# The store of a graph network's output, issued from ScalarE's queue in place of SyncE's

## The chip, the core and the metric

The kernel runs on one core of a Trainium2 chip. A core has TensorE (matrix products; PE in the profile, with its weight loads as PEld), VectorE (DVE), ScalarE (ACT), GpSimd (POOL) and SyncE (SP). Each works through its own queue of instructions in order, and they wait for one another through semaphores. Transfers between the chip's memory (DRAM) and the on-chip buffers run on 16 DMA engines; an engine of the core issues a transfer and goes on, and the transfer raises a semaphore when it has landed. The metric is the device time of one execution, in microseconds (us), median of several.

## The reference, cut to what matters

Sixty-four graphs of 256 nodes with 256 features each go through two layers; nothing connects one graph with another. All is in 32-bit floats.

```
layer 0:  h = gat(gat(x, adj, W1, a1), adj, W2, a2)      # gat: softmax over masked pair scores, times h W
          h = layernorm(x + h)
          x = layernorm(h + relu(h w_ff1 + b) w_ff2 + b)
layer 1:  attn = softmax(q k^T / sqrt(32)), 8 heads      # q, k = x Wq + bq, x Wk + bk
          out  = sum over relations r of (attn * (adj == r)) v_r
          x = layernorm(x + out Wo + bo)
          x = layernorm(x + gelu(x W1 + b1) W2 + b2)     # this is the output
```

`adj` has entries of 0 and 1 only, which the kernel makes use of, and checks: a general version of the whole computation follows behind a branch that these inputs don't take.

## The kernel before, in words

`binary` does the work. For each graph `b` the function `graph` makes a dictionary of small pieces of program, named by stage and step: G (the two graph-attention steps), F (the first feed-forward block), A (the attention), T (the end: projection, layernorm, second feed-forward block, last layernorm, store), L (loads). A piece is a few instructions. Which piece is run when is written out by hand: START fills a pipeline, PERIOD is run 58 times, each entry with a lag that says to which graph it belongs (in the period that starts graph n, `T.out/6` is the store of graph n-6), and END empties the pipeline. About seven graphs are in work at once. The order of pieces is the order of instructions on every engine; the scheduler adds none of its own.

Pieces and names that matter here:

- The store is `T.out`, function `store`, L1147: 256 KB from the tile `res_d` to the output, a transfer of 128 partitions x 2 rows of 1 KB. It stands in PERIOD behind `A.oc0` and ahead of `A.rz11`, `G.rzA`, `F.r3` and `F.r2`, and 6 times in END, the last three as `T.rbD:-3 T.rbD:-2 T.out:-3 T.rsD:-1 T.out:-2 T.nmD:-1 T.rbD:-1 T.out:-1`.
- `res_d` is written by `T.rbD` (`finished`, L613 and L614, VectorE), the weight and bias of the last layernorm. Its input `n_d` is written by ScalarE (`norm_to`, L591) in `T.nmD`.
- The pool `work` holds three buffers with the tag `res`. They are shared by `res_d` and by the scaled rows `res_a`, `res_b` and `res_c`, which GpSimd writes in `scaled`: L629 (times the weight, two instructions) and L634 (plus the bias). A buffer is written anew only when its last reader is done.
- GpSimd's order around the store is: the division by the sums of the softmax (L1057), `res_a` (`F.raA`, `F.rbA`), the root of the variance of the next layernorm (`T.rsC`, `rstd_c`, L583), and the sums of the hidden blocks of the feed-forward (`F.u0`, `F.u1`, `F.u3`, `F.u2`; tile `H_a`, L676), which TensorE multiplies at L796.
- ScalarE's order around the store is: the copies `oT` of the attention's result (`A.oc1`, `A.oc0`, L1095), the division `whz_A` (`G.rzA`, L923), the relu on the tile `hid_a` (`F.r3`, `F.r2`, L776), the copy `wh_B` (`G.wd1`, L864), the variance `var_c` (`T.lnC`, L579).
- All other transfers of the loop are issued by SyncE: the loads of `xT`, `adj` and `x` (L359, L363, L373), and the transposes through DRAM, which `turned` makes of a VectorE transpose of 32 x 32 blocks, a store `far...` (L546) and four loads (L553). Pieces named `dt`, `dm` and `mg` are these three steps. ScalarE issues two transfers in the whole kernel, both in the setup (L400).

What the weights of seven block products do in place of eight (`seven_products`) is of no account here.

Of the kernel before, what the change touches and what calls it, by code (L numbers as in the profile page):

```python
# [34 lines left out]
P = 128  # L35
# [175 lines left out]
def binary(ctx: ExitStack, tc: tile.TileContext, t, most, out: bass.AP):  # L211

    nc = tc.nc
# [409 lines left out]
    def scaled(do, stage, key, name, tiles, g, b):  # L623


        def times():
            tiles["res"] = work.tile([P, NT, D], F32, tag="res", name=f"res_{name}", bufs=3)
            for i in range(NT):
                nc.gpsimd.tensor_tensor(  # L629
                    tiles["res"][:, i, :], tiles["y"][:, i, :], rows[g], ALU.mult  # L630
                )

        def plus():
            nc.gpsimd.tensor_tensor(tiles["res"], tiles["res"], over_nodes(b), ALU.add)  # L634

        do[f"{stage}.ra{key}"], do[f"{stage}.rb{key}"] = times, plus

    def to_columns(do, stage, key, name, tiles, pairs=False):

        def out():
            sq = work.tile([P, 4, NT * KC * 32], F32, tag="sq", name=f"sq_{name}", bufs=2)
            flat = sq.rearrange("p b n -> p (b n)")
            if pairs:
                return flat, sq.rearrange("p b (t r k) -> p t k b r", t=NT, k=KC)
            return flat, flat

        def rows():
            y = tiles["y"]  # L650
            if pairs:
                return y.rearrange("p t (k b c) -> p t k b c", k=KC, b=4)
            return y.rearrange("p t (k b c) -> p b (t k) c", k=KC, b=4)

        def into():
            cols = work.tile([P, KC * N], F32, tag="cols", name=f"cols_{name}", bufs=3)
            if pairs:
                tiles["cols"] = cols.rearrange("p (n k) -> p k n", k=KC)
            else:
                tiles["cols"] = cols.rearrange("p (a t k r) -> p k t a r", a=4, t=NT, k=KC)  # L660
            return cols.rearrange("p (a n) -> p a n", a=4)

        turned(do, stage, key, f"y_{name}", P, rows, into, out)
# [14 lines left out]
    def combine(do, stage, key, name, tiles):  # L678


        def sums():
            s = tiles["S"] = work.tile([P, 4, P], F32, tag="S", name=f"S_{name}", bufs=3)
            cols = tiles["cols"]
            blocks = [block(cols, c, i) for i in range(NT) for c in range(KC)]
            sums = [s[:, n, :] for n in range(4)]
            if len(blocks[0].shape) == 3:
                sums = [n.rearrange("p (a r) -> p a r", a=4) for n in sums]
            add_sums(nc.gpsimd, blocks, sums, range(4))

        do[f"{stage}.s{key}"] = sums  # L690
# [435 lines left out]
    def graph(b, do, tiles):  # L1126
        a = gat(do, b, tiles)
        to_columns(do, "F", "A", f"a{b}", a)
        scaled(do, "F", "A", f"a{b}", a, "L0_gnn_g_ln1", "L0_gnn_b_ln1")
        combine(do, "F", "A", f"a{b}", a)  # L1130
        feed_forward(do, "F", f"a{b}", a, lambda: ff0, "r", AF.Relu)
        y = layernorm(do, "F", "B", f"b{b}", lambda: (a["ff"],), scalar=True)
        to_columns(do, "F", "B", f"y{b}", y, pairs=True)
        scaled(do, "F", "B", f"b{b}", y, "L0_gnn_g_ln2", "L0_gnn_b_ln2")
        combine(do, "F", "B", f"y{b}", y)
        heads = attention(do, b, projections(do, b, y), tiles)
        c = layernorm(do, "T", "C", f"c{b}", lambda: (heads["wo"], y["res"]))
        to_columns(do, "T", "C", f"c{b}", c)
        scaled(do, "T", "C", f"c{b}", c, "L1_gnn_g1", "L1_gnn_beta1")
        combine(do, "T", "C", f"c{b}", c)  # L1140
        feed_forward(do, "T", f"c{b}", c, ff1, "ge", AF.Gelu, b >= B - LAST)
        d = layernorm(
            do, "T", "D", f"d{b}", lambda: (c["ff"],), ("L1_gnn_g2", "L1_gnn_beta2"), True
        )

        def store():
            nc.sync.dma_start(out=out[b].rearrange("(t p) d -> p t d", p=P), in_=d["res"])  # L1147

        do["T.out"] = store

# [16 lines left out]
    with tc.manual_schedule(engines={E.PE, E.DVE, E.Activation, E.Pool, E.SP}):  # L1167
        for entry in START:
            piece, b = entry.split(":")
# [4 lines left out]
        for entry in END:  # L1174
            piece, b = entry.split(":")
# [306 lines left out]
```

## Time and profile before

| | |
|---|---|
| median of 3 runs | 2996.35 us (2993.79 to 2996.53) |
| profiled execution | 2993.21 us, of which the span from first to last instruction 2991.4 us |
| TensorE's granted clock | 0.995 of full speed |
| busy: TensorE / weight loads / VectorE / ScalarE / GpSimd | 99% / 89% / 87% / 75% / 76% |
| transfers | 449.27 MB in 401891 packets, 150 GB/s; SyncE's queue takes 46.7% of 16 engines' span |
| the store L1147 | 64 issues, 372 to 400 ns each, landing 2.1 to 4.0 us after issue, median 2.2 |

The page gives busy times by engine, the chain of work that ended last, the costliest groups of instructions and the issues of transfers. The timeline lists instructions of one engine in order of time: start and duration in us, engine, line, operation, the tile written and the tiles read, how many were merged, and in brackets how long the engine was idle before and whose work ended that. The view of a tile lists what writes and reads it, with durations as min/median/max in ns, and the time from issue to landing for a transfer. The list of waits says who waited for whom, how long in total, how often and how long at most.

### The profile page before, as it was taken

The page shows a single profiled execution, that of the slowest core. Times are in us where ns is not written, and L with a number is a line of the kernel's source. Part 1 is how long each engine was busy: PE and PEld are TensorE (multiplying, and loading weights), DVE is VectorE, ACT ScalarE, POOL GpSimd, SP SyncE. Part 2 cuts the span into 40 slices and gives each one's busy share as a digit, 9 for nine tenths or more (in the row PEclk, how much of TensorE's full clock was granted, in tenths as well). Part 3 has the DMA queues.
Part 4 walks back from the last instruction along what each step waited for, and adds up shares of the span by engine and source line. Part 5 has one row for each costly group of instructions (what it writes and reads, how often), then busy time and mean ns, then how long its engine had stood idle before and what let it go on. Part 6 is the DMA issues. An engine that isn't in the chain of part 4 may idle for free.

```text
span 2991.4 us, 75422 instructions
## 1 busy us (share of the span) xinstructions
PE 2947.1 (99%) x25662; PEld 2672.7 (89%) x25662; DVE 2599.5 (87%) x6247; ACT 2232.7 (75%) x6404; POOL 2281.8 (76%) x3455
## 2 busy tenths in 40 slices
PE   8999999999999999999999999999999999999997
PEld 7889999989999999999899899999999998898985
DVE  4888888888889888888898898898888898888885
ACT  3677787787787777777777777777877877877764
POOL 6777777777777777777778778777777787777785
PEclk9999999999999999999999999999999999999999
DMA  5545445445445444444444454454454444444442
GB/s 140 156 149 160 149 150 155 155 146 159 150 152 158 148 149 155 149 152 155 151 155 153 153 156 150 152 159 145 150 161 150 149 158 150 147 158 148 135 156 86
DMA packets 401891, 449.27 MB, mean 150 GB/s; under 512 B 41152, under 2 KB 342720, under 8 KB 401504
## 3 DMA queue, kind: packets, MB, share of 16 engines
q1 hardware_dynamic: 399984, 442.14, 46.7%
q8 instruction: 209, 3.42, 0.5%
q0 software_dynamic: 976, 1.72, 0.3%
q14 instruction: 178, 1.46, 0.2%
q10 hardware_dynamic: 544, 0.52, 0.1%
HBM read 242.90 MB, written 201.33 MB: 148 GB/s over the span
## 4 chain that ended last, share of the span: by engine, by line
PE 90%; POOL 3%; DVE 2%; DMA 2%; issue 1%; SPq 1%; ACT 0%; POOLq 0%; DVEq 0%; ACTq 0%
PE hX_a L758 8%; PE o L1082 8%; PE fX_a L796 7%; PE fX_c L796 7%; PE hX_c L758 7%; PE sc L1024 5%; PE wo L1103 4%; PE hY_a L758 4%; PE qX L967 4%; PE fY_c L796 4%; PE hY_c L758 4%; PE fY_a L796 3%; PE gat_a L930 3%; PE gat_b L930 3%; PE wh L847 3%; PE vX L991 3%
## 5 line engine op out<-in xcount | busy, mean ns | idle before, releaser
L1071 DVE SCALAR_TENSOR_TENSOR pm<-away,pm 128x512 f32<-128x512 uint8 x512 | 356.8, 708 | 4.4 <-DMA pm<-far_p 4.0
L542 DVE STREAM_TRANSPOSE p<-p 128x1024 f32<-128x1024 f32 x256 | 315.4, 1232 | 4.1 <-POOL p L1057 4.1
L1082 PE MATMUL o<-pm,v 128*32 128x256 f32 x4096 | 235.9, 381 | 0.0
L776 ACT ACTIVATE hid_c<-hid_c,col_L_gnn_b 128x256 f32<-128x256 f32 x512 | 231.5, 505 | 1.8 <-DVE hid_c L734 0.4
L776 ACT ACTIVATE hid_a<-hid_a,col_L_gnn_b_ff 128x256 f32<-128x256 f32 x512 | 224.2, 501 | 2.4 <-DVE hid_a L734 2.2
L796 PE MATMUL fX_a<-f_L_gnn_w_ff,hid_a 128*128 128x128 f32 x1536 | 203.8, 276 | 1.7 <-DVE acc_a L734 1.3
L796 PEld LDWEIGHTS fX_a<-f_L_gnn_w_ff,hid_a 128*128 128x128 f32 x1536 | 196.0, 192 | 10.5 <-DVE acc_a L734 2.4
L796 PE MATMUL fX_c<-f_L_gnn_W,hid_c 128*128 128x128 f32 x1536 | 203.5, 275 | 0.8 <-DVE acc_c L734 0.4
L1082 PEld LDWEIGHTS o<-pm,v 128*32 128x32 f32 x4096 | 126.6, 110 | 85.7 <-DVE pm L1071 1.1
L796 PEld LDWEIGHTS fX_c<-f_L_gnn_W,hid_c 128*128 128x128 f32 x1536 | 191.8, 192 | 5.6 <-DVE acc_c L734 0.6
L676 POOL TENSOR_TENSOR S_y<-cols_y 128x128 f32<-128x128 f32 x128 | 66.3, 518 | 121.1 <-DMA cols_y<-far_y_y 120.8
L770 ACT COPY hid_a<-hX_a 128x512 f32<-128x512 f32 x192 | 113.1, 589 | 60.5 <-PE hX_a L758 60.2
L1024 PE MATMUL sc<-kT,qT 32*128 32x256 f32 x2048 | 146.7, 400 | 2.5 <-DVE kT L988 2.4
L864 ACT COPY wh_B<-gat_a 128x258 f32<-128x258 f32 x124 | 46.3, 374 | 133.5 <-PE gat_a L930 133.5
L758 PE MATMUL hX_a<-S_a,f_L_gnn_w_ff 128*128 128x128 f32 x1024 | 144.1, 284 | 0.0
L758 PEld LDWEIGHTS hX_c<-cols_c,f_L_gnn_W 128*128 128x128 f32 x1024 | 131.0, 191 | 13.1 <-DVE hid_c L734 3.1
L758 PEld LDWEIGHTS hX_a<-S_a,f_L_gnn_w_ff 128*128 128x128 f32 x1024 | 124.0, 191 | 19.7 <-issue 19.2
L758 PE MATMUL hY_c<-S_c,f_L_gnn_W 128*128 128x128 f32 x1024 | 139.5, 279 | 0.0
L758 PE MATMUL hX_c<-cols_c,f_L_gnn_W 128*128 128x128 f32 x1024 | 135.3, 275 | 2.9 <-DVE hid_c L734 2.5
L796 PE MATMUL fY_a<-f_L_gnn_w_ff,H_a 128*128 128x128 f32 x1024 | 137.3, 277 | 0.8 <-DVE acc_a L809 0.6
L796 PE MATMUL fY_c<-f_L_gnn_W,H_c 128*128 128x128 f32 x1024 | 136.0, 276 | 1.5 <-POOL H_c L676 0.9
L758 PE MATMUL hX_a<-cols_a,f_L_gnn_w_ff 128*128 128x128 f32 x1024 | 136.0, 276 | 0.4 <-DMA cols_a<-far_y_a 0.3
(2844 smaller groups left out, 10562.5 us busy)
## 6 DMA issues: line engine op xcount, KB each, us to landing
far_p<-p SPq DMA_DIRECT2D x256, 512.0 KB, 3.0
pm<-far_p SPq DMA_DIRECT2D x1024, 128.0 KB, 3.0
adj<-in_adjT SPq DMA_DIRECT2D x64, 256.0 KB, 3.4
far_y_a<-sq_a SPq DMA_DIRECT2D x64, 256.0 KB, 2.1
cols_a<-far_y_a SPq DMA_DIRECT2D x256, 64.0 KB, 2.0
far_y_y<-sq_y SPq DMA_DIRECT2D x64, 256.0 KB, 2.0
cols_y<-far_y_y SPq DMA_DIRECT2D x256, 64.0 KB, 2.0
far_y_c<-sq_c SPq DMA_DIRECT2D x64, 256.0 KB, 2.0
```

The costliest lines, as they stand in the source:

```text
L542: nc.vector.transpose(to, rows)
L758: nc.tensor.matmul(ps[:, f * P : (f + 1) * P], weights()[0][:, factor, f * P : (f + 1) * P], left, start=start and f == 0, stop=f == FC // ...
L770: nc.scalar.copy(hidden(i, h), ps.rearrange("p (f n) -> p f n", n=P))
L776: nc.scalar.activation(tiles["hid"][:, f, :], tiles["hid"][:, f, :], func, bias=b1[:, f : f + 1])
L796: nc.tensor.matmul(ps, left[:, f, :], weights()[2][:, factor, f * P : (f + 1) * P], start=start and f == 0, stop=f == FC // 2 - 1, skip_gr ...
L847: nc.tensor.matmul(t["whp", j], tiles["xT"][:, c, nodes(j)], wx[:, c, :], start=(c == 0), stop=(c == KC - 1),)
L930: nc.tensor.matmul(ps, t["s"][:, j, nodes(i)], t["whz"][:, j, :width], start=(j == 0), stop=(j == NT - 1),)
L967: nc.tensor.matmul(ps[:, nodes(n)], w[:, factor, :], right, start=start and n == 0, stop=n == 1, skip_group_check=True,)
L1024: nc.tensor.matmul(t["sc", g, hh][:, i, :], qkv["q"][hd, g, nodes(i)], qkv["k"][hd, g, :], start=True, stop=True,)
L1071: nc.vector.scalar_tensor_tensor(pm[:, 1], tiles["away"].rearrange("p (a n) -> p a n", a=4), 0.0, pm[:, 0], ALU.is_equal, ALU.mult,)
L1082: nc.tensor.matmul(ps[hh * DH : (hh + 1) * DH, :], qkv["v"][:, j, d0 : d0 + DH], t["pm", (g, hh)][:, r].rearrange("p a (j t r) -> p j t a ...
L1103: nc.tensor.matmul(t["wo"][:, i, :], t["oT"][:, c, nodes(i)], late["wo"][:, c, :], start=(c == 0), stop=(c == KC - 1),)
```

## The change

The store is issued by ScalarE. Its place in the orders START, PERIOD and END, the tile that it reads and everything else stay.

```diff
@@ -1144,7 +1144,7 @@
         def store():
-            nc.sync.dma_start(out=out[b].rearrange("(t p) d -> p t d", p=P), in_=d["res"])
+            nc.scalar.dma_start(out=out[b].rearrange("(t p) d -> p t d", p=P), in_=d["res"])
 
         do["T.out"] = store
```

## The prediction, made before the change was run

> **What bounds the kernel now.** I read the page's table of engines and its chain first, then one period of the loop engine by engine.
>
> ```profile
> PE 2947.1 (99%) x25662; PEld 2672.7 (89%) x25662; DVE 2599.5 (87%) x6247; ACT 2232.7 (75%) x6404; POOL 2281.8 (76%) x3455
> PE 90%; POOL 3%; DVE 2%; DMA 2%; issue 1%; SPq 1%; ACT 0%; POOLq 0%; DVEq 0%; ACTq 0%
> ```
>
> TensorE is busy for 99% of the span and carries 90% of the chain that ended last: only what makes a matmul start later costs time. The output's 64 issues follow one another at a median of 45.12 us (58 in the written period, 6 in END); I take the period whose output is issued at 1526.45 us, and call that moment 0. First SyncE's queue in the timeline, then the view of the tile `out`:
>
> ```profile
> 1518.88 0.47 SPq L373 DMA_DIRECT2D x<-in_x  x1
> 1526.45 0.38 SPq L1147 DMA_DIRECT2D out<-res_d  x1
> 1528.39 0.34 SPq L546 DMA_DIRECT2D far_p<-p  x1
> ```
>
> ```profile
> L1147 SPq DMA_DIRECT2D out<-res_d x64: 372/384/400, 215.3 to 2984.6; - x64
> ...
>   POOL res_a L629: 0.4, 2
> ...
> DMA to landing us min/median/max: 2.1/2.2/4.0
> ```
>
> SyncE finishes with x at 1519.35 and stands until VectorE has written `res_d` at 1526.42. The output lands 2.15 us after its issue, but up to 4.0 in some periods, and GpSimd's `res_a` (L629) is seen to wait for it: the ring of three `res` buffers gives `res_a` the buffer that the output is read from. In one period the landing at 3.97 is followed by `res_a` at 4.04, so the wake-up takes 0.07. Now ScalarE and GpSimd around the same place:
>
> ```profile
> 1529.01 0.47 ACT L1095 ACTIVATE oT<-o,col_bv 128x256 f32<-128x256 f32 x1 [0.41 <-PE o L1082]
> 1529.38 0.90 ACT L923 ACTIVATE whz_A<-wh_A,grz_A 128x258 f32<-128x258 f32 x2
> ...
> 1532.85 0.37 ACT L864 COPY wh_B<-gat_a 128x258 f32<-128x258 f32 x1 [0.98 <-PE gat_a L930]
> ```
>
> ```profile
> 1530.29 1.41 POOL L629 TENSOR_TENSOR res_a<-y_a,row_L_gnn_g_ln 128x256 f32<-128x256 f32 x2
> 1531.78 1.27 POOL L634 TENSOR_TENSOR res_a<-res_a,row_L_gnn_b_ln 128x512 f32<-128x512 f32 x1
> 1534.40 0.70 POOL L583 TENSOR_TENSOR rstd_c<-var_c,neghalf 128x2 f32<-128x2 f32 x1 [1.35 <-ACT var_c L579]
> ...
> 1537.76 1.27 POOL L676 TENSOR_TENSOR H_a<-hid_a,H_a 128x512 f32<-128x512 f32 x1
> ```
>
> ```profile
> 1539.08 0.97 PEld L796 LDWEIGHTS fY_a<-f_L_gnn_w_ff,H_a 128*128 128x128 f32 x8
> ```
>
> GpSimd goes `res_a`, `rstd_c`, then three sums `H_a` without a gap. The third ends at 1539.03, and TensorE's weight load for `fY_a` starts 0.05 later, in all 58 periods that I compared. So GpSimd's chain has no slack against TensorE, and the idle 1.35 us ahead of `rstd_c` is the only cushion behind `res_a`.
>
> **What the change does, part by part.**
>
> *SyncE loses 64 issues of 0.384 us and the stand before them.* Value: nothing. The next entry of its queue, `far_p` at 1528.39, waits for VectorE's transpose of `p` (1527.14 + 1.23 = 1528.37), not for the output. A gain is bounded by what TensorE loses in the whole periodic part beyond 45.11 us a period: 6.5 us, nearly all of it at `qX<-cols_y`, a transfer issued 20 us earlier.
>
> The Trainium skill's "DMA: Bandwidth & Descriptors", section "Issuing engines are not separate DMA queues", says that a second issuing engine saves only the sequencer's issue time. By that the sum would be 0, since SyncE stands idle anyway; the row of `res_a` says that it isn't the whole sum.
>
> *ScalarE gains 64 issues.* In its order the output stands behind the second `oT` copy (piece A.oc0) and ahead of `whz_A`. Its own two transfers in the setup took 0.44 and 0.49 us. Its queue starts a semaphore instruction 5 ns after the start of an activation still running (1534.029 after 1534.024), so I take the issue at 1529.05, +2.60, while `oT` runs. Neither semaphore holds it: `res_d` was ready at -0.03, and SyncE's separate wait for the transfer's counter (63 instructions) took 17 ns each. Queued behind it are `whz_A`, the relu on `hid_a`, and `wh_B`. `whz_A` and the relu slide by 0.1 to 0.5 us; TensorE loads `whz_A` only at 1531.56 (it was done at 1530.28), and the 0.98 us idle ahead of `wh_B` takes up the rest. Cost: nothing. Without that cover it would be 0.5 us a period, 28 us.
>
> *The output lands later, and `res_a` with it.* The issue moves from 0 to +2.60. For `rstd_c` to be on time, `res_a` may start up to 3.83 + 1.35 = 5.18, so the output must land by 5.18 - 0.07 = 5.11, or 2.51 us after ScalarE's issue. Alone it would land at 2.60 + 2.15 = 4.75: 0.36 us to spare. But it is no longer alone. The transfers' view from 1526 to 1532 in forty slices of 0.15 us:
>
> ```profile
> DMA  0000000006999930000005999989891100400000
> ```
>
> Output (0.9 us, first), then `far_p` (1.3 us, from 2.7 to 4.05). Moved, the output's data would start at 3.5 inside `far_p`'s. If the 16 engines share them with nothing lost, both are done at 2.75 + 1.3 + 0.85 = 4.9 and the output lands 0.4 later, at 5.3: `res_a` is 0.2 too late. If sharing costs the output nothing, 0. I take the middle, 0.1 us for an ordinary period.
>
> The same page, section "Queues, rings and completion order", has the engines go round-robin between queue rows packet by packet. By that the two share; the 36 ordinary periods below would cost 7 us, not 4.
>
> *Collisions with instruction fetches.* In 18 of 58 periods the output now lands at 3.3 to 4.0, since a 16 KB fetch (the page's instruction queue q8, 209 of them) sits on one of its engines; the cushion hides all of them now. `far_p`, whose time slot the output moves into, lands over 0.35 us late in 20 of 58 periods; about 13 of these are its own, and 8 or 9 more fetches start just behind it, where the output's tail will be. I take 22 periods. A collided output lands about 1.46 later than 2.15 (mean of the 18), hence at 6.2: 1.1 too late; `far_p`'s collisions cost it only 0.65, hence 5.4: 0.3. I take 0.8.
>
> *The end.* END puts T.out of graph 62 ahead of the last normalisation (T.nmD:-1).
>
> ```profile
> 2981.64 3.38 SPq L1147 DMA_DIRECT2D out<-res_d  x3
> ...
> 2981.99 1.17 ACT L591 ACTIVATE n_d<-H_c,mv_d,rstd_d 128x256 f32<-128x256 f32 x2 [0.31 <-POOL mv_d L587]
> ...
> 2983.19 0.70 DVE L613 TENSOR_TENSOR n_d<-n_d,row_L_gnn_g 128x512 f32<-128x512 f32 x1
> ```
>
> ScalarE would now stand until `res_d` of 62 is written (2983.14), issue (0.4), and start the last `n_d` at 2983.55, not 2981.99. VectorE takes `n_d` up as soon as it is there: +1.6 us on the end. The other four of END find `res_d` written, or ScalarE idle (next work at 2859.61, 2914.12, 2976.92): nothing.
>
> **Sum.** A late `res_a` shifts `rstd_c`, the `H_a` sums and `fY_a` one for one, and TensorE has no idle time in which to make it good, so each period is longer by it. 36 x 0.1 + 22 x 0.8 + 1.6 = 3.6 + 17.6 + 1.6 = 22.8 us. The profiled execution took 2993.21 (span 2991.4 and 1.8 around it), 3.1 below the median of the runs, 2996.35. On the median: 2996.35 + 22.8, about **3019 us**, +0.8%.
>
> **Rivals.**
>
> *The spare holds (not slower).* If sharing costs the output nothing and collisions keep it below 2.51 us after its issue, `res_a` is on time everywhere and only the end is left: 2996.35 + 1.6 = 2998. For it: 0.36 us of spare, and 39 of 58 outputs now land at 2.14 to 2.23. Against: `far_p` is in flight in every period, and 18 collided landings above 3.3. It decides at exactly 2.51 us from issue to landing.
>
> *ScalarE issues only when `oT` has ended.* Then +0.47 us on every landing: 36 x 0.57 + 22 x 1.27 + 1.6 = 50 us, 3046. Against it: the 5 ns above. For it: no transfer in this trace is issued beside a running activation.
>
> *SyncE's freedom pays (faster).* `x`, `far_p` or the loads would have to start earlier, but each has its own wait; at most 6.5 us, 2990.
>
> *The move changes nothing but a name.* If the two queues fed one order of transfers, `far_p` would go first in full and the output land at 4.05 + 0.85 + 0.4 = 5.3, the upper end of the ordinary period: 36 x 0.2 + 17.6 + 1.6 = 26 us, inside the forecast.
>
> **How the numbers follow.** 0.2%, or 6 us, is about what a measurement of this kernel can tell from no change. Forecast (+6 to +45): 0.60. Issue after `oT`, or worse sharing (+40 to +65): 0.14. The spare holds: 0.22. Faster: 0.04. All but the ends: 2994 takes in the spare's case, 3056 the late issue's. Slower 0.74, same 0.22, faster 0.04.
>
> **What would show it.** In the profile after: the output on ScalarE's queue 0.05 us behind the start of the second `oT`; GpSimd waiting for `out<-res_d` at `res_a` by about 1 us in nearly all periods, not 0.4 us in two; a shorter or vanished idle time ahead of `rstd_c`; matmuls of `fY_a` waiting for GpSimd's `H_a`; a period above 45.12 us, unevenly so, longest where the output lands beyond 3 us. I am wrong if landing stays below 2.5 us after issue, if `whz_A` or `wh_B` becomes the wait, or if TensorE loses its time elsewhere.

## The result, and the profile after

The changed kernel takes 3029.36 us (median of 4 runs, 3026.07 to 3030.91) against 2996.44 us before (2993.79 to 2996.76): the ratio is 1.0113, with a 95% interval of 1.0101 to 1.0125, or 33 us. It is slower, as forecast, and by ten microseconds more than the forecast of 3019 us. The profiled execution took 3029.0 us with a span of 3027.2 us, 35.8 more than the span before.

The page of the changed kernel, busy times and chain:

```profile
PE 2968.7 (98%) x25662; PEld 2676.3 (88%) x25662; DVE 2608.2 (86%) x6247; ACT 2242.0 (74%) x6404; POOL 2283.9 (75%) x3455
PE 73%; POOL 9%; ACT 6%; DMA 5%; DVE 5%; issue 2%; SPq 1%; DVEq 0%; POOLq 0%; ACTq 0%
```

GpSimd's busy time is what it was (2281.8 us before), but its share of the chain has gone from 3% to 9%, and that of transfers from 2% to 5%. ScalarE's has gone from 0% to 6% as well, so the page alone doesn't tell whether TensorE waits for the landing or for ScalarE; the experiments do. The view of the tile `out`:

```profile
L1147 ACTq DMA_DIRECT2D out<-res_d x64: 378/378/448, 218.7 to 3020.2; - x64
...
  POOL res_a L629: 107.0, 58
  POOL res_c L629: 2.4, 1
  POOL res_b L629: 2.0, 1
...
DMA to landing us min/median/max: 2.1/2.8/4.9
```

GpSimd waits for the store in each of the 58 periods, 107 us in all, where it was 0.4 us in two. One ordinary period, ScalarE and then GpSimd:

```profile
1590.73 0.47 ACT L1095 ACTIVATE oT<-o,col_bv 128x256 f32<-128x256 f32 x1 [0.39 <-PE o L1082]
1590.79 0.38 ACTq L1147 DMA_DIRECT2D out<-res_d  x1
1591.22 0.91 ACT L923 ACTIVATE whz_A<-wh_A,grz_A 128x258 f32<-128x258 f32 x2
...
1594.57 0.38 ACT L864 COPY wh_B<-gat_a 128x258 f32<-128x258 f32 x1 [0.85 <-PE gat_a L930]
```

```profile
1593.68 1.42 POOL L629 TENSOR_TENSOR res_a<-y_a,row_L_gnn_g_ln 128x256 f32<-128x256 f32 x2 [1.63 <-DMA out<-res_d]
1595.18 1.28 POOL L634 TENSOR_TENSOR res_a<-res_a,row_L_gnn_b_ln 128x512 f32<-128x512 f32 x1
1596.41 0.70 POOL L583 TENSOR_TENSOR rstd_c<-var_c,neghalf 128x2 f32<-128x2 f32 x1
...
1599.78 1.26 POOL L676 TENSOR_TENSOR H_a<-hid_a,H_a 128x512 f32<-128x512 f32 x1
```

The store is issued 0.06 us behind the start of the second `oT`. ScalarE's own work slides by 0.1 us, and its idle time ahead of `wh_B` is still 0.85. GpSimd's idle time has moved: 1.63 us ahead of `res_a`, none ahead of `rstd_c`, where it was 1.35. The cushion is used up, and 0.3 more. TensorE's weight load of this period shows that rest:

```profile
1601.10 0.97 PEld L796 LDWEIGHTS fY_a<-f_L_gnn_w_ff,H_a 128*128 128x128 f32 x8 [0.25 <-POOL H_a L676]
```

Why the landing takes 2.8 us and not 2.2 is seen in the transfers' view from 1587 to 1596 us (40 slices of 0.225 us, q10 is ScalarE's queue):

```profile
DMA  0000010000300000058999989981000387788959
...
q1 hardware_dynamic: 656, 1.00, 32.9%
q10 hardware_dynamic: 272, 0.26, 8.0%
```

There is one block of 2.3 us, `far_p` and the output together, in which the two separate blocks of before (0.9 and 1.3 us) have run into one. Inside the block they don't alternate. The same view from 1590.8 to 1592.28 us, and from there to 1593.3 us (records, MB, share of the engines):

```profile
q1 hardware_dynamic: 127, 0.52, 89.7%
...
q10 hardware_dynamic: 272, 0.26, 70.5%
q1 hardware_dynamic: 17, 0.00, 1.7%
```

In the first stretch 127 of the 128 records of `far_p` start and none of the output; all of the output's follow in the second. So it is in every ordinary period (the 40 whose store lands within 2.9 us of its issue): at most one record of `far_p` starts after the output's first. The output's data begin 1.50 us after its issue, where they began 0.91 us after it before, and take 0.9 us in both; `far_p` lands 2.69 us after its issue, and 2.67 before (medians). The output is late by the 0.6 us for which its data wait for those of `far_p`.

In the period that begins 47 us earlier the store lands 4.67 us after its issue, and GpSimd stands twice as long:

```profile
1548.28 1.42 POOL L629 TENSOR_TENSOR res_a<-y_a,row_L_gnn_g_ln 128x256 f32<-128x256 f32 x2 [3.48 <-DMA out<-res_d]
```

The end of the program, ScalarE and its queue:

```profile
3015.57 1.91 ACTq L1147 DMA_DIRECT2D out<-res_d  x2
...
3017.52 1.17 ACT L591 ACTIVATE n_d<-H_c,mv_d,rstd_d 128x256 f32<-128x256 f32 x2 [1.92 <-DVE res_d L614]
```

The last `n_d` waits 1.92 us for the `res_d` of the graph before it, to which it has no tie but the queue.

I cut the span at VectorE's residual add behind the attention (L571, the one that writes `wo`) of graph 0 and of graph 57. Up to the first 136.8 us (135.75 before): +1.0, which has nothing to do with the change, since no store has been issued by then and this stretch was 135.0 to 137.5 us in the eleven profiles of this study. Between them 2600.6 us (2571.8): +28.8, the loop. From there 289.9 us (283.9): +6.0, of which about 1.0 are the two last stores of the loop and about 5 the six of END.

### The profile page after: what moved, and what is told of

The parts are those of the page before. It is cut to its first block, busy times and chain, and to the rows that moved or that the text cites. A ratio compares the mean times of both kernels' runs of the same rounds, so it can differ in the third digit from the quotient of the medians.

```text
span 3027.2 us, 75417 instructions
## 1 busy us (share of the span) xinstructions
PE 2968.7 (98%) x25662; PEld 2676.3 (88%) x25662; DVE 2608.2 (86%) x6247; ACT 2242.0 (74%) x6404; POOL 2283.9 (75%) x3455
## 4 chain that ended last, share of the span: by engine, by line
PE 73%; POOL 9%; ACT 6%; DMA 5%; DVE 5%; issue 2%; SPq 1%; DVEq 0%; POOLq 0%; ACTq 0%
PE hX_c L758 7%; PE fX_c L796 6%; PE fX_a L796 5%; PE hX_a L758 5%; PE o L1082 4%; PE qX L967 4%; PE hY_c L758 3%; PE sc L1024 3%; PE wh L847 3%; PE gat_b L930 3%; PE vX L991 3%; POOL H_a L676 3%; PE fY_a L796 3%; DMA out<-res_d 3%; ACT p L1045 3%; PE hY_a L758 3%
## 5 line engine op out<-in xcount | busy, mean ns | idle before, releaser
L629 POOL TENSOR_TENSOR res_a<-y_a,row_L_gnn_g_ln 128x256 f32<-128x256 f32 x128 | 91.0, 732 | 107.0 <-DMA out<-res_d 107.0
L796 PEld LDWEIGHTS fY_a<-f_L_gnn_w_ff,H_a 128*128 128x128 f32 x1024 | 127.5, 191 | 29.4 <-POOL H_a L676 25.7
```

Of the source, the lines that this page charges most:

```text
L629: nc.gpsimd.tensor_tensor(tiles["res"][:, i, :], tiles["y"][:, i, :], rows[g], ALU.mult)
L796: nc.tensor.matmul(ps, left[:, f, :], weights()[2][:, factor, f * P : (f + 1) * P], start=start and f == 0, stop=f == FC // 2 - 1, skip_gr ...
```

## The experiments

All ratios are to the kernel before, run on the same chip beside them. **Late buffer** is the theory of the prediction: the store lands later, so GpSimd gets the buffer for `res_a` later, and with it the `H_a` sums and TensorE. **ScalarE's own time** is the first rival: 64 issues of 0.38 us on an engine that is busy for 75% of the span are 24 us, close to the loss. **The second queue** is the other: that a transfer lands later because it is on ScalarE's queue.

| run | what is changed | us | ratio (95% interval) |
|---|---|---|---|
| e1_res4 | changed kernel, four `res` buffers | 2994.4 | 1.0012 (1.0003 to 1.0021) |
| e2_sp_late | SyncE's store, 2.3 us later in its order | 3016.4 | 1.0082 (1.0068 to 1.0096) |
| e3_act_early | ScalarE's store, earlier in its order | 2995.2 | 1.0011 (1.0002 to 1.0020) |
| e4_act_probe | before, and a small transfer on ScalarE | 2992.7 | 1.0004 (0.9995 to 1.0013) |
| e5_end_only | ScalarE's store in END alone | 2996.6 | 1.0016 (1.0007 to 1.0025) |
| e7_half | changed kernel, half the bytes | 3006.1 | 1.0048 (1.0034 to 1.0061) |
| e8_act_later | ScalarE's store behind `G.rzA` | 3022.6 | 1.0102 (1.0087 to 1.0118) |
| e9_twice | changed kernel, the bytes twice | 3076.5 | 1.0276 (1.0260 to 1.0291) |
| e10_early_sp_end | e3, with SyncE's store in END | 2991.1 | 0.9996 (0.9987 to 1.0005) |

**e1_res4: take away the wait.**

```diff
-            tiles["res"] = work.tile([P, NT, D], F32, tag="res", name=f"res_{name}", bufs=3)
+            tiles["res"] = work.tile([P, NT, D], F32, tag="res", name=f"res_{name}", bufs=4)
...
-            do, "T", "D", f"d{b}", lambda: (c["ff"],), ("L1_gnn_g2", "L1_gnn_beta2"), True
+            do, "T", "D", f"d{b}", lambda: (c["ff"],), ("L1_gnn_g1", "L1_gnn_beta1"), True
```

The rows of `L1_gnn_g2` and `L1_gnn_beta2` are no longer loaded either, which makes the room.

> ScalarE issues the store as in the changed kernel, but the ring of res buffers has four in place of three. To make room the last layernorm uses the weight and bias rows of the layernorm before it (the output is that of other weights, the work is the same). Theory of the late buffer: GpSimd no longer waits for out<-res_d at res_a, the period goes back to 45.12 us, and what is left is the stand of ScalarE at the end, 1.6 us: 2996.4 + 1.6 = 2998 (ratio to before 1.0005). Rival, ScalarE's own time (0.38 us of issue in each of 64 graphs is what TensorE loses): nothing changes, 3020 to 3029 (1.008 to 1.011).

1.0012; the 1.0005 that was expected lies in the interval. In its profile the store lands as late as in the changed kernel (2.8 us), nobody waits for it, and GpSimd's cushion is back:

```profile
1530.95 1.41 POOL L629 TENSOR_TENSOR res_a<-y_a,row_L_gnn_g_ln 128x256 f32<-128x256 f32 x2
...
1535.05 0.70 POOL L583 TENSOR_TENSOR rstd_c<-var_c,neghalf 128x2 f32<-128x2 f32 x1 [1.35 <-ACT var_c L579]
```

The loop takes 2572.1 us, as before. What is left is ScalarE's stand at the end: the last `n_d` still waits 1.92 us for `res_d`, and from the residual add of graph 63 to the end it takes 42.9 us, against 41.2 before. The wait for the buffer carries the rest.

**e2_sp_late: the lateness without ScalarE.**

```diff
-... A.oc0/4 T.out/6
+... A.oc0/4
-... A.dm11/3 F.raA/2 ...
+... A.dm11/3 T.out/6 F.raA/2 ...
```

(on the kernel before: SyncE issues)

> SyncE issues the store, but in the period it stands behind A.dm11, the store of p, that is 2.3 us later in SyncE's order; END is as before. Theory of the late buffer: its data follow those of far_p, it lands about 5.3 us after the old moment of issue, 0.2 past the limit of 5.11, and some 20 collisions with fetches add 0.8 each: 58 x 0.2 + 14 = 25, about 3021 (1.008). Rival, ScalarE's own time: ScalarE issues nothing, 2996 (1.000). Rival, the second queue (a transfer on ScalarE's queue lands later because it is another queue): 2996 to 3000 (1.000 to 1.001).

1.0082. SyncE's queue alone makes the same wait:

```profile
L1147 SPq DMA_DIRECT2D out<-res_d x64: 372/436/1684, 218.8 to 3012.4; - x64
...
  POOL res_a L629: 106.1, 58
...
DMA to landing us min/median/max: 2.1/3.0/5.0
```

Issued behind `far_p` in the same queue, the store lands 0.24 us beyond the limit of 5.11 in an ordinary period; from ScalarE's queue it was 0.25. It is issued 0.23 us before the second `oT` starts, in the changed kernel 0.06 us after, and lands 2.8 us behind that start in both. Engine and queue don't matter: the landing follows the end of `far_p`'s data.

**e3_act_early: ScalarE without the lateness.**

```diff
-... F.hk4/2 F.r0/2 ...
+... F.hk4/2 T.out/6 F.r0/2 ...
-... A.oc0/4 T.out/6
+... A.oc0/4
```

(on the changed kernel)

> ScalarE issues the store, but in the period it stands behind F.hk4 in place of behind A.oc0, about 2.1 us earlier in ScalarE's order; END is as in the changed kernel. Theory of the late buffer: issue at about +0.46, landing by 2.7 to 3.2, far below 5.11, collisions hidden again: the period is 45.12 us, and only the end's loss of 5.6 us is left: 3002 (1.002). Rival, ScalarE's own time: as the changed kernel, 3020 to 3029 (1.008 to 1.011). The second queue: 3002 as well, with landing at 2.75 after issue in place of 2.15.

1.0011; the interval just reaches the 1.002 that was expected. The loop takes 2571.6 us, as before. On ScalarE's queue too the landing is 2.2 us when `far_p` isn't there:

```profile
L1147 ACTq DMA_DIRECT2D out<-res_d x64: 377/378/447, 215.3 to 2987.8; - x64
...
DMA to landing us min/median/max: 2.1/2.2/4.6
```

So the second queue isn't slow of itself.

**e4_act_probe: ScalarE's issue by itself.**

```diff
             nc.sync.dma_start(out=out[b].rearrange("(t p) d -> p t d", p=P), in_=d["res"])
+            probe = far.tile([16, P], F32, tag="probe", name=f"probe_{b}", bufs=8)
+            nc.scalar.dma_start(out=probe, in_=ident[:16, :])
```

> SyncE issues the store as before, and ScalarE issues a transfer of 8 KB from a constant to a scratch buffer in DRAM at the same place, which nothing waits for. Theory of the late buffer: ScalarE's issue of 0.38 us is hidden in its 0.98 us of idle time ahead of wh_B, 2996 to 2998 (1.000 to 1.0005). Rival, ScalarE's own time: 64 x 0.38 = 24 us, 3020 (1.008).

1.0004, no difference that can be told. ScalarE's 64 issues, 0.31 us each in this kernel, would be 20 us; at this place they cost nothing.

**e5_end_only: the end by itself.**

```diff
+            queue = nc.sync if b < B - lags else nc.scalar
-            nc.sync.dma_start(out=out[b].rearrange("(t p) d -> p t d", p=P), in_=d["res"])
+            queue.dma_start(out=out[b].rearrange("(t p) d -> p t d", p=P), in_=d["res"])
```

> SyncE issues the 58 stores of the periods, ScalarE the six of END. Theory of the late buffer: the periods stay at 45.12 us; in END ScalarE comes to the store later than SyncE did, GpSimd waits for it at res_b and res_c (2.0 and 2.4 us in the changed kernel, part of it hidden), and the last n_d is 1.6 late: +3 to +6 us (1.001 to 1.002). If END is as the prediction had it, +1.6 (1.0005).

1.0016, 5 us (2 to 7), as expected and more than the prediction's 1.6. Its loop takes 2573.7 us and its tail (the stretch behind the second cut) 287.4, +3.5. One profile's tail is only known to a microsecond or so: with END as it was before, it is 283.6 in e10 and 285.2 in e4.

**e7_half and e9_twice: less and more to wait for.**

```diff
-            nc.scalar.dma_start(out=out[b].rearrange("(t p) d -> p t d", p=P), in_=d["res"])
+            nc.scalar.dma_start(out=out[b][:P], in_=d["res"][:, 0, :])
```

> As the changed kernel, but only the first 128 rows of each graph's output are stored (128 KB in place of 256 KB; the other half of the output is left out). Theory of the late buffer, with shared engines: the data end 0.43 us earlier, landing about 2.3 us after issue, +4.9 on the old scale, ahead of the limit of 5.11: ordinary periods are back at 45.12 us, some 18 periods with a fetch on one of the output's engines still lose 0.6 each, END 3: +10 to +16 (1.0035 to 1.005). Rival, ScalarE's own time: the issue is the same, 3020 to 3029 against 2996 (1.008 to 1.011).

1.0048. The store lands 2.34 us after its issue in an ordinary period, just short of the limit of 2.5, and all 43 ordinary periods lose nothing; 15 with a late landing lose 0.86 each, 12.9 us together.

```diff
+            twice = far.tile([P, NT, D], F32, tag="twice", name=f"twice_{b}", bufs=8)
+            nc.scalar.dma_start(out=twice, in_=d["res"])
             nc.scalar.dma_start(out=out[b].rearrange("(t p) d -> p t d", p=P), in_=d["res"])
```

> As the changed kernel, but ahead of the store ScalarE issues the same 256 KB once more to a scratch buffer in DRAM. Theory of the late buffer, with shared engines: far_p and both copies share the engines, data end 0.85 us later, the store lands at +6.2, 1.1 us past the limit in an ordinary period and 1.9 in some 18 with a fetch: 40 x 1.1 + 18 x 1.9 + 6 = 84 us, 3080 against 2996 (1.028), median period 46.2 us. Rival, ScalarE's own time: one more issue of 0.38 us in 64 graphs, 24 us more than the changed kernel, 3054 (1.019), median period 45.8.

1.0276, 83 us. The median period is 46.2 us, as the late buffer has it, and not 45.8.

```profile
  POOL res_a L629: 154.5, 58
...
DMA to landing us min/median/max: 2.4/3.1/5.0
```

ScalarE isn't free of this run: behind the second issue (0.62 us, median, where it is 0.38 in the changed kernel) it stands idle ahead of `whz_A`, 37 us in all. But what GpSimd starts `rstd_c` too late, counted from the end of `var_c`, sums to 73.4 us over the 56 stores between the two cuts, and the loop lost 76.7, so at most the 3.3 us that are left are ScalarE's.

Nothing, 0.25 and 1.0 us lost in an ordinary period for 128, 256 and 512 KB: below the limit no price, above it the full one.

**e8_act_later: a miss.**

```diff
-... A.oc0/4 T.out/6
+... A.oc0/4
-... A.rz11/3 G.rzA/1 F.rbB/4 ...
+... A.rz11/3 G.rzA/1 T.out/6 F.rbB/4 ...
```

> As the changed kernel, but the store stands behind G.rzA in place of behind A.oc0: ScalarE issues it 0.8 us later, at +3.4. Theory of the late buffer, with shared engines: far_p's data have ended when the output's begin, it lands 2.2 us after its issue in place of 2.75, at +5.55 in place of +5.37, so an ordinary period is 0.45 us late in place of 0.25: 58 x 0.2 = 11 us more than the changed kernel, ratio to before 1.0145 to 1.0155 (collisions may differ). If the delay after issue is the second queue's own, landing stays at 2.75 after issue, +6.15, 1.05 late: 46 us more, 1.026.

1.0102, which neither had: the move didn't delay the issue at all. Its timeline on ScalarE:

```profile
1544.24 0.47 ACT L1095 ACTIVATE oT<-o,col_bv 128x256 f32<-128x256 f32 x1 [0.39 <-PE o L1082]
1544.25 0.38 ACTq L1147 DMA_DIRECT2D out<-res_d  x1
1544.61 0.90 ACT L923 ACTIVATE whz_A<-wh_A,grz_A 128x258 f32<-128x258 f32 x2
```

In the order of instructions the store stands behind both `whz_A`, yet it is issued 0.36 us before the first of them starts. It lands at the same moment as in the changed kernel (2.81 us behind the start of `oT` in both), and so it says nothing about a later landing; e9 does.

**e10_early_sp_end: both losses undone.** The order of e3, and in `store`:

```diff
+            queue = nc.scalar if b < B - lags else nc.sync
```

> ScalarE issues the 58 stores of the periods early, behind F.hk4, and SyncE the six of END as before. Theory of the late buffer: nothing is left to wait for, the time is that of the kernel before, 2996 (0.9995 to 1.0005). If ScalarE's issues cost something of their own that the early place only hid in part, it is above 1.001.

0.9996: 58 stores on ScalarE's queue at no cost that can be told. It doesn't beat the kernel before either: by the interval SyncE's freedom is worth 4 us at most, and nothing is seen of it.

## Why the prediction was right, and where its sizes were off

*ScalarE's issues cost nothing.* Right: e1, e4 and e10. The issue was expected at +2.60 on the prediction's scale, and came at 2.55 + 0.06 = +2.61; it doesn't wait for `oT` to end, so that rival falls.

*SyncE's relief is worth nothing.* Right: e10 at 0.9996.

*The store lands late, `res_a` waits, the cushion of 1.35 us is used up, and the rest comes one for one out of TensorE.* Right, and shown by taking away one link at a time: the wait (e1), the lateness (e3), ScalarE (e2). In the changed kernel a period grows by 0.98 us for each us that `res_a` is late beyond the cushion (a line through the 57 periods, correlation 0.93). What GpSimd starts `rstd_c` too late sums to 28.4 us between the two cuts, where the loop lost 28.8.

*An ordinary period loses 0.1 us.* Too small, and the first step that failed. The step took "the middle" between sharing without loss (0.2) and sharing that costs the output nothing (0). The landing came at 2.61 + 2.75 = +5.36, a little later than the late end of that range, 5.3, and the 40 ordinary periods lose 0.25 each: 9.9 us in place of 3.6. The mechanism was another one too. The two transfers don't share the engines: `far_p` goes first and the output after it, as the prediction's last rival had it ("The move changes nothing but a name"). Sharing without loss would end the output at the same time; that the upper end came near is luck as far as the mechanism goes. No alternation is seen in the trace's records, so the round-robin that the prediction set beside this step isn't seen either; how many records would make one packet, no run shows. The view of before already had `far_p`'s block at eights and nines, so little was left for a second transfer. The step also read that view 0.15 us too early: `far_p`'s block begins at 1529.30, that is at +2.85 and not 2.7 (the records say 2.79 to 4.21). So the upper end would have been 5.4 by sharing and 5.45 by the rival.

*Collisions: 22 periods at 0.8.* 18 periods at 1.14: 20.6 us in place of 17.6. Each of the 18 has an instruction fetch (queues q8 and q14) running while the store is in flight, of the 40 others eight, at its edges. The middle between the output's own collisions (1.1) and `far_p`'s (0.3) was again the wrong place; the first came from the rows of the same transfer and was right. That 22 periods were taken and 18 came made up for part of it.

*The end costs 1.6 us.* Too small. ScalarE's stand is there (42.9 us in place of 41.2 for the last stretch in e1). What failed is the sentence "The other four of END find `res_d` written, or ScalarE idle: nothing". It asked only whether ScalarE has to wait, not whether the store then comes later for those who wait for its buffer. It does: one is issued 5.6 us later, counted from the residual add of graph 59, another lands 4.89 us after its issue, and GpSimd waits 2.0 us at `res_b` and 2.4 at `res_c`. With four buffers (e1) this part is gone. How the 5 us divide over the six stores stays open: e5's END showed other waits than the changed kernel's, and one tail is known to a microsecond or so.

Sum: 9.9 + 20.6 of the periods, of which the cut between graph 0 and graph 57 shows 28.8, and about 5 of END, against 3.6 + 17.6 and 1.6.

## What to carry to other kernels

A transfer moved to another queue has two ends. Ask when it is issued there, and then who waits for its landing, above all the engine that will write the same buffer next. That a move is free for the engine that issues says nothing about that. Take the slack of that waiter from the profile (here 1.35 us, of which the move left 0.36 spare had the store been alone) and assume that a transfer issued into the data of another one lands only when both are through. Where a slower end of a range has a row for the very same operation, don't halve it.

## What the runs showed of the hardware

- ScalarE's queue issues a transfer ahead of activations that stand before it in the order: 0.36 us before the start of the first of two `whz_A` in e8, and 0.40 us before the start of a copy `hid_a` in e3 (1526.05 against 1526.45). In e8 it followed by 0.01 us the start of `oT`, which had waited for TensorE, in e3 by 0.03 us the end of `res_d`, which it reads. So what held it was the last unfulfilled wait at or ahead of it, as far as these two places show. Moving a transfer by two activations in the order therefore moved it by nothing. The Trainium skill, "Advanced Engine Details and Errata", section "Sequencer and Instruction Queues", has the sequencer push an engine's instruction into a queue and go on; the rows agree.
- Two transfers on two queues went one after the other: 256 KB took 2.15 us to land alone and 2.75 when issued 0.67 us behind `far_p` (512 KB) on the other queue, its data beginning 1.50 us after issue in place of 0.91. Issued 0.39 us behind `far_p` on the same queue (e2) it landed at the same moment, 2.8 us behind the start of `oT`.
- The Trainium skill, "Perfetto Trace Analysis", section "DMA Optimizations", says that it may make sense to give inputs to one issuing engine and outputs to another. Here only the output's store was moved, the stores of the transposes stayed with the loads on SyncE: that was 1.1% slower at the old place in the order, and no different at an earlier one (0.9996, with the six stores of END on SyncE).
